# Four edits to the order of work around the second layer of a four-layer graph network

## The chip, the core and the metric

The kernel runs on one core of a Trainium2 chip. The metric is the device time of one execution in microseconds (us); the kernel before takes 2077.56 us (median of three runs, 2076.71 to 2078.34). A core has five engines, each with its own queue of instructions: TensorE (PE, matrix products; its weight loads are listed as PEld), VectorE (DVE), ScalarE (ACT), GpSimd (POOL) and SyncE (SP), which issues most of the transfers (DMAs). [...]

## The reference

Four layers on x of 128 graphs x 64 nodes x 256 features, each followed by a residual sum and a layer normalisation over the features:

```python
x = _layernorm(x + _L0_gnn_ref(x, adj, W, a))             # attention over the adjacency
x = _layernorm(x + _L1_gnn_ref(x, ..., adj, src, dst))    # attention over 512 edges
x = _layernorm(x + _L2_gnn_ref(x, adj, W1, b1, ...))      # the layer of this change
x = _layernorm(x + _L3_gnn_ref(x, adj, Wg0, ..., Wih, Whh, bih, bhh))  # two graph products, then LSTMs
```

Layer 2 (counted from 0) is two dense layers, each with a normalisation over all 8192 rows:

```python
agg = jnp.einsum('nm,bmd->bnd', A_hat, features)
h = jax.nn.relu(_batchnorm(agg.reshape(-1, d) @ W1.T + b1, g1, be1))   # 256 -> 512
out = _batchnorm(h @ W2.T + b2, g2, be2)                               # 512 -> 256
```

## The kernel before, in words

The 8192 rows lie in 16 blocks of 512 (q = 0 to 15), features on the 128 partitions. `Aq(q)` holds a block's input to layer 2 and later half of its hidden values and its result; `Z[q]` holds the other half (`hidden(q, m)`, m = 0 to 3).

*The end of layer 1.* Edge scores of two blocks are gathered in one PSUM bank. `l1_softmax` (line 362) adds a bias, runs two scans for the segment maximum, subtracts and exponentiates (line 375); `l1_sums` (378) runs two more scans; `l1_weights` (383) transposes both results on TensorE (389), takes a reciprocal (395), multiplies (397) and scatters by indirect DMA from GpSimd (401). For the last two blocks these are called one after another after the main loop. `v_a`, `v_b` and `v_c` (410 to 463) then finish layer 1 block by block (line 422 products, 436 output projection, 100 normalisation on GpSimd, 456 neighbour product) while layer 2's first product already fills TensorE (`up`, 737, and `up_job`, 909).

*Jobs of seven products.* Both products of layer 2 are partly done by a scheme of seven products in place of eight (`Seven`, 789). A job covers two blocks and two output parts. It needs sums of its inputs: `tile_sums` (885) and, in a given order, `sums_in_order` (895): t3 on GpSimd, t1 on VectorE in place, t2 and t4 on GpSimd. `factor` (778) says which product uses which. A job's products go in the order 1, 6, 5, 2, 3, 7; the fourth (`tail`, 847) is issued within the next job. `use` (820) takes the products out of PSUM on three engines: lines 823, 827, 829 and 832 ScalarE, 825, 835, 838 and 841 VectorE, 833 and 839 GpSimd. Some products go on in a bank that has just been read (`at`, 803): product 7 waits for line 825, product 4 for line 838, product 2 for line 823, product 3 for line 827. In the second product a job has two terms and so 14 matrix products, each of which is two passes in the profile: 28 passes.

*Statistics and normalisation.* `bn_stats` runs over each finished part; `normalisation` (719) aggregates, takes a reciprocal root by a power on GpSimd (86) and forms scale and shift. `relu` (977) applies them to a block's part in place, on ScalarE.

*The second product.* `first` (1004) does blocks 0 to 3 plainly, k after k, with `beside` (1060) putting rectifications and the sums of blocks 4 and 5 between. Jobs 4, 6, 8, 10 and 12 follow (1090). `prepare(q + 2)` (1021) is stepped through during job q: it rectifies blocks q+2 and q+3 and makes their sums. Blocks 14 and 15 are done plainly at the end (1092 to 1110), and line 1111 adds two bias vectors for the last layer, which come by the transfers of lines 951 and 952.

*The last layer's start.* `gcn` (1216) is a generator for half a group: scale the block (1226), twice transpose, add the residual and normalise (1244, 1250, 100), a neighbour product (1212), two products with the first weights (1282), two with the second (1294) and a last neighbour product whose rectified result goes to `H` (1305 VectorE, 1306 ScalarE). Parts 0 and 1 make the group that the first LSTM step (1331) reads; parts 2 and 3 come after. A list of part numbers (1638) says whose step is issued next.

*What sets the order.* `given` (110) issues what it is handed after the last instruction of each of the four compute engines that was issued through `given` before: it fixes the order of each engine's queue. What isn't issued through it is placed by the scheduler of the framework, by priority and readiness, so that an edit can also move instructions that it does not name.

Of the kernel before, what the change touches and what calls it, by code (L numbers as in the profile page):

```python
# [12 lines left out]
OP = mybir.AluOpType  # L13
# [13 lines left out]
NQ = 16  # L27
# [14 lines left out]
def kernel(ctx: ExitStack, tc: tile.TileContext, i, out):  # L42
    nc = tc.nc
# [66 lines left out]
    def given(do, *args, **more):  # L110
        traced = nc.cur_bb.bb.instructions
        first = len(traced)
        with ExitStack() as order:
            for e in latest.values():
                order.enter_context(tc.issue_after(e))
            r = do(*args, **more)
# [13 lines left out]
    with ExitStack() as two:  # L130
# [355 lines left out]
        ends = su.tile([P, 2, E], F32, name="ends")  # L486
# [195 lines left out]
        for q in range(NQ):  # L682
            S = q // BPS - 1 if q % BPS == 0 else -1
# [15 lines left out]
                    setup.pop(0)()  # L699
        sums(q)  # L700
        S = NQ // BPS - 1
        for do in (l1_softmax, l1_sums, l1_weights):
            do(S)
        ph.close()


# [12 lines left out]
        def normalisation(scale, shift, st, gamma, beta, m):  # L719

            mv = wb.tile([P, 2], F32, name="bn_mv", bufs=4)
            c = slice(m, m + 1)
            nc.vector.bn_aggr(mv, st[:, m, :, :].rearrange("p q s -> p (q s)"))
            rsqrt(scale[:, c], mv[:, 1:2], 1)
            nc.vector.tensor_mul(scale[:, c], scale[:, c], gamma[:, c])
            nc.vector.tensor_mul(shift[:, c], mv[:, 0:1], scale[:, c])
            nc.vector.tensor_sub(shift[:, c], beta[:, c], shift[:, c])
# [123 lines left out]
                if self.done:  # L851
                    self.order(self.done)

        late = []

        def seven(job, feed=iter(())):
            rest = late.pop(0).tail() if late else iter(())
            job.product(1)
            next(feed, None)
            job.product(6)  # L860
            if len(job.terms) > 1:
                next(rest, None)
            next(feed, None)
            job.product(5)
            next(rest, None)
            next(feed, None)
            job.product(2)
            for _ in rest:
                pass
            next(feed, None)  # L870
            job.product(3)
            job.counted(0, 0)
            next(feed, None)
            job.product(7)
            job.counted(0, 1)
            next(feed, None)
            late.append(job)

# [6 lines left out]
        def tile_sums(b):  # L885

            t2, t3, t4 = rooms[next(rooms_at) % len(rooms)]
            t1 = b(0, 1)
            nc.gpsimd.tensor_tensor(t3, b(1, 1), t1, OP.subtract)
            nc.vector.tensor_sub(t1, t1, b(0, 0))  # L890
            nc.gpsimd.tensor_tensor(t2, b(1, 1), t1, OP.subtract)
            nc.gpsimd.tensor_tensor(t4, b(1, 0), t2, OP.subtract)
            return [t1, t2, t3, t4]

        def sums_in_order(b):
# [10 lines left out]
        def inputs(q):  # L906
            return lambda k, n: Aq(q + n)[:, k * QT:(k + 1) * QT]

        def up_job(q, g, T, done=None, **more):
# [3 lines left out]
            seven(Seven([(a, [SW[0][:, n, g] for n in range(4)], inputs(q), T)],  # L913
                        lambda m: b1[:, 2 * g + m:2 * g + m + 1], dst, stats, done, **more))

        T = {}

        def one(q):
            return lambda: up_block(q)
# [12 lines left out]
        q = NQ - LAST - 1  # L932
# [32 lines left out]
        ends = range(NQ - LAST, NQ, 2)  # L965
        T = {ends[0]: tile_sums(inputs(ends[0]))}
# [1 line left out]
        T[ends[1]] = tile_sums(inputs(ends[1]))  # L968

        def finish(g):  # L970
            return lambda: [normalisation(sc1, sh1, st1, g1, be1, 2 * g + m) for m in range(2)]

        for g in range(2):
            for q in ends:
                up_job(q, g, T[q], finish(g) if q == ends[-1] else None, order=given)

        def relu(q, m):
            h = hidden(q, m)
            nc.scalar.activation(h, h, AF.Relu, bias=sh1[:, m:m + 1], scale=sc1[:, m:m + 1])  # L979

        def down(q, m, p_, ks):
            for k in ks:
# [21 lines left out]
        def first(k, feed):  # L1004
            for q in range(LAST):
                for m in range(M2):
                    if k == 0:
                        pz[q, m] = pbank()
                    given(down, q, m, pz[q, m], [k])
                    if k == M1 - 1:  # L1010
                        given(nc.vector.bn_stats, st2[:, m, q, :], pz[q, m])
                        if m:
                            for n in range(M2):
                                given(leave, q, n, pz[q, n])
                    elif k == 0 and m == 0 and q in (0, 1):
                        next(rest, None)
                next(feed, None)

# [18 lines left out]
        def ready(q):  # L1037
            for k in range(M1):
                for n in range(2):
                    given(relu, q + n, k)  # L1040
# [16 lines left out]
        for q in range(LAST):  # L1057
            given(relu, q, 0)

        def beside(k):  # L1060
            q0 = LAST
            early = [(q0 + n, j) for j in (2 * (k // 2), 2 * (k // 2) + 1) for n in range(2)]
            for q in range(LAST):
                if k == 0:
                    given(relu, q, 1)
                if k == 1:
                    given(relu, q, 2)
                    given(relu, q, 3)
                else:
                    if k < 3:  # L1070
# [661 lines left out]
```

## Time and profile before

| what | us |
|---|---|
| time, median of three | 2077.56 |
| the profiled execution: whole | 2077.86 |
| the profiled execution: first to last instruction (span) | 2076.1 |
| end of the last `first` products, start of job 4 (line 813) | 693.77 |
| start of the plain products of blocks 14 and 15 (line 983) | 765.37 |
| the memset of line 1179, the end of layer 2 | 784.17 |
| first LSTM product (line 1331) | 818.61 |

The page of the profile lists busy time per engine; the other views used are busy time in chosen stretches, the waits of one engine in a stretch (engine, tile and line, what it waited for, us in total, times, longest), the chain of waits that ended last (start, us, engine and line), and the timeline (start, us, engine, line, operation, output<-input, count, and in brackets the idle time before with what ended it). A wait is only dear where the waiting engine is the one that the end of the program hangs on.

### The profile page before, as it was taken

The page shows a single profiled execution, that of the slowest core. Times are in us where ns is not written, and L with a number is a line of the kernel's source. Part 1 is how long each engine was busy: PE and PEld are TensorE (multiplying, and loading weights), DVE is VectorE, ACT ScalarE, POOL GpSimd, SP SyncE. Part 2 cuts the span into 40 slices and gives each one's busy share as a digit, 9 for nine tenths or more (in the row PEclk, how much of TensorE's full clock was granted, in tenths as well). Part 3 has the DMA queues.
Part 4 walks back from the last instruction along what each step waited for, and adds up shares of the span by engine and source line. Part 5 has one row for each costly group of instructions (what it writes and reads, how often), then busy time and mean ns, then how long its engine had stood idle before and what let it go on. Part 6 is the DMA issues. An engine that isn't in the chain of part 4 may idle for free.

```text
span 2076.1 us, 31444 instructions
## 1 busy us (share of the span) xinstructions
PE 1964.1 (95%) x11583; PEld 1374.2 (66%) x11583; DVE 1193.1 (57%) x2683; ACT 968.7 (47%) x1852; POOL 809.6 (39%) x961
## 2 busy tenths in 40 slices
PE   5999999998899998999999999999999999999997
PEld 4666667675454335587687587677587677586675
DVE  7455665554556445574456674456674456543556
ACT  2766666665245433443343543343543343543333
POOL 1123343343525434273545243345343345224254
PEclk8999999999999998999999999999999999999998
DMA  5444343332202015451142532032522032301012
GB/s 133 80 66 64 77 77 54 55 54 44 34 21 59 31 71 209 148 192 62 60 153 69 172 121 97 11 126 73 170 95 81 1 113 75 128 1 76 1 60 73
DMA packets 235961, 170.68 MB, mean 82 GB/s; under 512 B 150561, under 2 KB 213537, under 8 KB 232481
## 3 DMA queue, kind: packets, MB, share of 16 engines
q1 hardware_dynamic: 233952, 166.72, 28.6%
q8 instruction: 91, 1.49, 0.3%
q0 software_dynamic: 1024, 1.05, 0.2%
q10 hardware_dynamic: 832, 0.92, 0.1%
q14 instruction: 62, 0.50, 0.1%
HBM read 107.82 MB, written 60.82 MB: 81 GB/s over the span
## 4 chain that ended last, share of the span: by engine, by line
PE 58%; DVE 9%; POOL 4%; issue 2%; ACT 1%; DMA 1%; SPq 0%; POOLq 0%; DVEq 0%; ACTq 0%
PE l L1474 27%; PE l L1439 9%; PE l L1331 8%; PE pz L813 4%; PE pz L742 2%; PE g L1294 2%; PE pz L983 2%; PE g L1212 1%; PE g L1282 1%; DVE cell L1418 1%; DVE gate L1417 1%; DVE ln_st L95 1%; DVE kept L1495 1%; ACT A L979 1%; POOL gate L1497 0%
## 5 line engine op out<-in xcount | busy, mean ns | idle before, releaser
L1474 PE MATMUL l<-xs,wx 128*128 128x256 f32 (+1 forms) x896 | 276.8, 399 | 4.9 <-DVE gate L1493 3.9
L1474 PE MATMUL l<-hs,wh 128*128 128x256 f32 (+1 forms) x896 | 275.0, 399 | 3.1 <-DVE hs L1368 3.1
L86 POOL TENSOR_TENSOR ln_rs<-ln_rs,mhalf 128x2 f32<-128x2 f32 (+2 forms) x98 | 84.0, 858 | 437.2 <-DVE ln_rs L98 425.9
L1489 ACT ACTIVATE kept<-l 128x256 f32<-128x256 f32 (+1 forms) x224 | 88.6, 403 | 339.7 <-PE l L1474 338.5
L1474 PE MATMUL l<-H,wx 128*128 128x256 f32 (+1 forms) x672 | 210.2, 401 | 3.7 <-DVE gate L1502 3.7
L1474 PE MATMUL l<-hid,wh 128*128 128x256 f32 (+1 forms) x672 | 208.7, 399 | 0.0
L1474 PEld LDWEIGHTS l<-xs,wx 128*128 128x128 f32 x896 | 168.8, 190 | 49.3 <-POOL st L100 4.1
L1474 PEld LDWEIGHTS l<-hs,wh 128*128 128x128 f32 x896 | 169.4, 190 | 45.3 <-DVE hs L1368 5.3
L1439 PE MATMUL l<-H,wx 128*128 128x256 f32 (+1 forms) x768 | 187.9, 403 | 6.2 <-DVE H L1404 6.2
L1507 ACT ACTIVATE gate<-gate,bias 128x512 f32<-128x512 f32 (+1 forms) x280 | 170.7, 657 | 37.1 <-DVE gate L1498 31.1
L1439 PEld LDWEIGHTS l<-H,wx 128*128 128x128 f32 x768 | 146.8, 193 | 46.4 <-DVE H L1404 10.4
L1331 PE MATMUL l<-H,wih 128*128 128x512 f32 x384 | 167.9, 598 | 2.6 <-issue 2.6
L357 ACT ACTIVATE u<-z 128x1024 f32<-128x1024 f32 x128 | 130.4, 1025 | 63.3 <-PE z L355 62.3
L1474 PEld LDWEIGHTS l<-H,wx 128*128 128x128 f32 x672 | 126.0, 190 | 38.6 <-DVE gate L1502 7.6
L1474 PEld LDWEIGHTS l<-hid,wh 128*128 128x128 f32 x672 | 127.2, 190 | 32.0 <-issue 2.6
L1331 PEld LDWEIGHTS l<-H,wih 128*128 128x128 f32 x384 | 73.3, 192 | 93.2 <-issue 86.2
L1497 POOL TENSOR_TENSOR gate<-gate,kept 128x256 f32<-128x256 f32 (+1 forms) x84 | 65.1, 775 | 159.1 <-DVE kept L1495 159.1
L329 DVE TENSOR_TENSOR qs<-m,qs 64x256 fp32r<-64x256 f32 x128 | 54.0, 422 | 109.7 <-ACT qs L328 107.6
L1372 POOL TENSOR_TENSOR hs<-hid 128x256 f32<-128x256 f32 (+1 forms) x28 | 26.0, 930 | 200.2 <-DVE hid L1401 116.3
L355 PE MATMUL z<-gath_r,qs 128*128 128x512 f32 x256 | 99.9, 478 | 0.1
L1426 ACT ACTIVATE gate<-cell 128x512 f32<-128x512 f32 (+1 forms) x88 | 58.6, 666 | 81.0 <-DVE cell L1418 57.5
L1491 DVE TENSOR_TENSOR gate<-l,kept 128x256 f32<-128x256 f32 (+1 forms) x112 | 49.1, 438 | 71.4 <-ACT gate L1507 43.7
(340 smaller groups left out, 3831.4 us busy)
## 6 DMA issues: line engine op xcount, KB each, us to landing
wx<-sums SPq DMA_DIRECT2D x9, 2048.0 KB
wh<-sums SPq DMA_DIRECT2D x9, 1792.0 KB
way<-st SPq DMA_DIRECT2D x54, 256.0 KB
st<-way SPq DMA_DIRECT2D x216, 64.0 KB
xin<-in_x SPq DMA_DIRECT2D x16, 512.0 KB
ld<-table SPq DMA_DIRECT2D x16, 512.0 KB
x_dram<-y SPq DMA_DIRECT2D x16, 512.0 KB
x2r<-x_dram SPq DMA_DIRECT2D x32, 256.0 KB
```

What stands on the lines that cost most here:

```text
L86: nc.gpsimd.tensor_tensor(dst, dst, mhalf[:, :n], OP.pow)
L329: nc.vector.tensor_sub(qs[ro, s, :], pq[r, :D], qs[r, s, :].bitcast(F32))
L355: nc.tensor.matmul(z[:, k, :], L1[q]["qs"][c][:, s, k * P:(k + 1) * P], gath_r, start=True, stop=True)
L357: nc.scalar.activation(u, z, AF.Relu)
L813: nc.tensor.matmul(self.bank[at], lhs, rhs, start=first and n == 0, stop=n == len(self.terms) - 1, skip_group_check=True)
L1331: nc.tensor.matmul(b, wih1[:, k, mw * P:(mw + 1) * P], Hw[:, k], start=k == 0, stop=k == KD - 1)
L1426: nc.scalar.activation(tiles["g"][m], cell[:, m], AF.Tanh)
L1439: nc.tensor.matmul(one, w.raw[0][:, k, at, m, :], inp(r, 0, k)[:, g], start=k == 0, stop=k == KD - 1)
L1474: nc.tensor.matmul(self.banks[j], lhs, rhs, start=src == 0, stop=src == 1)
L1489: nc.scalar.activation(self.keep(j), b, AF.Copy)
L1497: e.tensor_tensor(t[0][:, 1], t[0][:, 1], k[5], OP.add)
L1507: given(lambda: nc.scalar.activation(dst, dst, f, bias=b))
```

## The change

1. The last `l1_softmax` and `l1_sums` are issued through `given`, and so are the four instructions of `tile_sums`; so the softmax stands ahead of the input sums.
2. `normalisation` is made of two parts, `variance` (aggregate, root) and `affine` (scale and shift). For the first product's statistics, `finish` no longer runs them at once but puts the parts of two columns into a list, `aside`, from which `two_aside` issues two at a time at later points.
3. Rectifications: those of blocks 0 to 3, part 0, move into the last `up_job`; `prepare(q)` now makes the sums of blocks q and q+1 and rectifies blocks q+2 and q+3, so rectifications are two jobs ahead; those of blocks 6 and 7 move into `beside`. `ready` is gone.
4. The list that orders the steps of parts 0 to 3 in the last layer changes.

```diff
-        for do in (l1_softmax, l1_sums, l1_weights):
-            do(S)
+        given(l1_softmax, S)
+        given(l1_sums, S)
+        l1_weights(S)
...
+        def halves(scale, shift, st, gamma, beta, m):
             mv = wb.tile([P, 2], F32, name="bn_mv", bufs=4)
             c = slice(m, m + 1)
+            return [lambda: variance(mv, scale[:, c], st, m), lambda: affine(mv, scale, shift, gamma, beta, c)]
+
+        def variance(mv, dst, st, m):
             nc.vector.bn_aggr(mv, st[:, m, :, :].rearrange("p q s -> p (q s)"))
-            rsqrt(scale[:, c], mv[:, 1:2], 1)
+            rsqrt(dst, mv[:, 1:2], 1)
+
+        def affine(mv, scale, shift, gamma, beta, c):
             nc.vector.tensor_mul(scale[:, c], scale[:, c], gamma[:, c])
...
+        def two_aside():
+            for part in aside[:2]:
+                given(part)
+            del aside[:2]
...
             job.counted(0, 0)
+            two_aside()
             next(feed, None)
             job.product(7)
             job.counted(0, 1)
+            two_aside()
...
-            nc.gpsimd.tensor_tensor(t3, b(1, 1), t1, OP.subtract)
-            nc.vector.tensor_sub(t1, t1, b(0, 0))
-            nc.gpsimd.tensor_tensor(t2, b(1, 1), t1, OP.subtract)
-            nc.gpsimd.tensor_tensor(t4, b(1, 0), t2, OP.subtract)
+            given(nc.gpsimd.tensor_tensor, t3, b(1, 1), t1, OP.subtract)
+            given(nc.vector.tensor_sub, t1, t1, b(0, 0))
+            given(nc.gpsimd.tensor_tensor, t2, b(1, 1), t1, OP.subtract)
+            given(nc.gpsimd.tensor_tensor, t4, b(1, 0), t2, OP.subtract)
...
         def finish(g):
-            return lambda: [normalisation(sc1, sh1, st1, g1, be1, 2 * g + m) for m in range(2)]
+            def done():
+                both = [halves(sc1, sh1, st1, g1, be1, 2 * g + m) for m in range(2)]
+                aside.extend(h[n] for n in range(2) for h in both)
+            return done
...
+        def early_relus():
+            yield
+            for q in range(LAST):
+                yield
+                given(relu, q, 0)
...
-                    elif k == 0 and m == 0 and q in (0, 1):
+                    elif k == 0 and m == 0 and q < 3:
                         next(rest, None)
...
+            later = [(k, n) for k in range(M1) for n in range(2)]
+
+            def one():
+                k, n = later.pop(0)
+                given(relu, q + 2 + n, k)
             for g in range(2):
-                for k in range(2):
-                    for n in range(2):
-                        given(relu, q + n, 2 * g + k)
-                    if k == 0:
-                        yield
...
                 T = sums_in_order(b)
-                yield next(T)
+                next(T)
+                one()
+                yield
                 terms[q].append((a, [SW[1][:, n, g] for n in range(4)], b, next(T)))
+                one()
                 if g == 0:
-                    yield
+                    one()
                 yield
+            one()
+            yield
+            one()
+            one()
...
+                if k >= 2:
+                    given(relu, q0 + 2 + q % 2, 2 * (k - 2) + q // 2)
+                two_aside()
...
-            down_job(q, prepare(q + 2) if q + 2 < NQ - 2 else ready(q + 2))
+            down_job(q, prepare(q + 2) if q + 2 < NQ - 2 else iter(()))
...
-    for n in [0, 0, 0, 1, 0, 1, 0, 1, 0, 1, 0, 1, 2, 0, 1, 0, 1, 3, 1, 2, 2, 1, 3, 3]:
+    for n in [0, 0, 0, 1, 1, 0, 1, 0, 0, 1, 0, 0, 1, 1, 0, 2, 1, 3, 1, 1, 2, 2, 3, 3]:
```

More of the change, by code (lines that the diff above doesn't have):

```diff
@@ L717, with normalisation @@
         sc2, sh2 = (const.tile([P, M2], F32, name=n) for n in ("sc2", "sh2"))
-        def normalisation(scale, shift, st, gamma, beta, m):
+        def normalisation(*args):
+            for part in halves(*args):
+                part()
+        def halves(scale, shift, st, gamma, beta, m):
             mv = wb.tile([P, 2], F32, name="bn_mv", bufs=4)
             c = slice(m, m + 1)
+            return [lambda: variance(mv, scale[:, c], st, m), lambda: affine(mv, scale, shift, gamma, beta, c)]
+        def variance(mv, dst, st, m):
             nc.vector.bn_aggr(mv, st[:, m, :, :].rearrange("p q s -> p (q s)"))
-            rsqrt(scale[:, c], mv[:, 1:2], 1)
+            rsqrt(dst, mv[:, 1:2], 1)
+        def affine(mv, scale, shift, gamma, beta, c):
             nc.vector.tensor_mul(scale[:, c], scale[:, c], gamma[:, c])
@@ L852, in tail @@
                     self.order(self.done)
-        late = []
+        late, aside = [], []
+        def two_aside():
+            for part in aside[:2]:
+                given(part)
+            del aside[:2]
         def seven(job, feed=iter(())):
@@ L907, in inputs, with up_job @@
             return lambda k, n: Aq(q + n)[:, k * QT:(k + 1) * QT]
-        def up_job(q, g, T, done=None, **more):
+        def up_job(q, g, T, done=None, feed=iter(()), **more):
             a = lambda m, k: w1[:, k, (2 * g + m) * P:(2 * g + m + 1) * P]
@@ L913, in up_job @@
             seven(Seven([(a, [SW[0][:, n, g] for n in range(4)], inputs(q), T)],
-                        lambda m: b1[:, 2 * g + m:2 * g + m + 1], dst, stats, done, **more))
+                        lambda m: b1[:, 2 * g + m:2 * g + m + 1], dst, stats, done, **more), feed)
         T = {}
@@ L970, in finish @@
         def finish(g):
-            return lambda: [normalisation(sc1, sh1, st1, g1, be1, 2 * g + m) for m in range(2)]
-        for g in range(2):
-            for q in ends:
-                up_job(q, g, T[q], finish(g) if q == ends[-1] else None, order=given)
+            def done():
+                both = [halves(sc1, sh1, st1, g1, be1, 2 * g + m) for m in range(2)]
+                aside.extend(h[n] for n in range(2) for h in both)
+            return done
         def relu(q, m):
@@ L979, in relu @@
             nc.scalar.activation(h, h, AF.Relu, bias=sh1[:, m:m + 1], scale=sc1[:, m:m + 1])
+        def early_relus():
[3 more added lines that the diff above has]
+                given(relu, q, 0)
+        for g in range(2):
+            for q in ends:
+                last = q == ends[-1]
+                up_job(q, g, T[q], finish(g) if last else None, feed=early_relus() if last and g else iter(()),
+                       order=given)
         def down(q, m, p_, ks):
@@ L1031, in prepare @@
                 T = sums_in_order(b)
-                yield next(T)
+                next(T)
+                one()
+                yield
                 terms[q].append((a, [SW[1][:, n, g] for n in range(4)], b, next(T)))
+                one()
                 if g == 0:
-                    yield
[L1037 to L1040, printed above, removed]
+                    one()
                 yield
+            one()
+            yield
+            one()
+            one()
         def down_job(q, feed):
@@ L1056 @@
         rest = late.pop(0).tail()
-        for q in range(LAST):
-            given(relu, q, 0)
         def beside(k):
```

## The prediction, made before the changed kernel ran

> **What bounds the kernel now.** I read the page first, then the busy times by stretch, then what TensorE waited for in each stretch of layer 2, then the chain of waits through one job, and last the timelines around single places.
>
> ```profile
> PE 1964.1 (95%) x11583; PEld 1374.2 (66%) x11583; DVE 1193.1 (57%) x2683; ACT 968.7 (47%) x1852; POOL 809.6 (39%) x961
> ```
>
> TensorE is the bound, and the change removes no product: the order of the built programs shows the same matrix products, a few of them in another place. So it can only win or lose idle TensorE time, and the slow matmuls that follow idle time. Busy time by stretch (us, each engine, then the granted clock) says where that lies:
>
> ```profile
> 520.00:560.00 40.00, 31.76 (x215) 16.05 (x216) 21.10 (x35) 10.18 (x16) 20.93 (x20) 0.96 0.25 39
> ...
> 695.00:725.00 30.00, 25.79 (x56) 10.77 (x54) 17.52 (x26) 18.04 (x27) 17.84 (x15) 0.94 0.12 48
> 725.00:755.00 30.00, 26.26 (x56) 11.06 (x56) 15.22 (x20) 14.56 (x22) 16.94 (x15) 0.94 0.15 62
> ...
> 785.00:820.00 35.00, 28.24 (x338) 19.52 (x337) 22.09 (x61) 13.07 (x22) 10.77 (x18) 0.84 0.66 232
> ```
>
> 8.2 us idle around the last softmax, some 4 us in each 30 us of the second product's jobs, 6.8 us in the first blocks of the last layer, all with the clock below 1. The waits of TensorE (us in total, times, longest) in the stretches 518 to 665, 665 to 784 and 784 to 880 name the causes:
>
> ```profile
> PE m L389 <- ACT e L375: 4.9, 1, 4.9
> PE m L456 <- POOL y L100: 2.2, 2, 1.5
> PE pz L813 <- DVE wq L838: 1.9, 1, 1.9
> ...
> PE pz L813 <- POOL wv L116: 4.4, 2, 2.2
> PE pz L813 <- POOL Z L116: 4.4, 2, 2.2
> PE pz L983 <- ACT Z L979: 0.6, 1, 0.6
> ...
> PE l L1331 <- issue: 2.6, 1, 2.6
> ```
>
> The four waits of 2.2 us are one per job. The chain of waits through one of them (start, us):
>
> ```profile
> 717.15 0.44 ACT A L829
> 717.59 0.15 issue
> 717.74 2.93 ACT A L979 x4
> 720.66 0.07 issue
> 720.73 1.28 POOL seg L116
> 722.01 0.02 issue
> 722.04 1.75 DVE A L116
> 723.79 0.07 issue
> 723.86 1.28 POOL wv L116
> ```
>
> Four rectifications, then GpSimd, VectorE and GpSimd by turns, and only then TensorE: the next job's sums start when this job is nearly over.
>
> [...] after two of the four 2.2 us waits the next 14 matmul passes take 7.99 us, after the other two 6.29 us, where the undisturbed pace is 0.429 us each (6.0 us). [...] the in-place subtraction takes 0.69 us alone and 1.74 us beside the GpSimd sum of line 839.
>
> **The change part by part.** Times are on the clock of the profiled run (span 2076.1, whole run 2077.86 us).
>
> *Last softmax.* Before, VectorE runs the first scan to 526.09, then sits 1.77 us behind a subtraction of the input sums (527.86, waiting for GpSimd's lb), then the second scan (1.22), then a subtraction of 1.57 us beside GpSimd; the exponential ends at 531.95. In the changed order that subtraction stands behind both softmax scans and their sums. Second scan 526.1 to 527.4, subtraction 0.69 to 1.1, exponential 0.63: about 529.0, so the first transposes come 3.0 us earlier. The further scans (1.23, 1.22) put the next transposes at about 531.4 against 534.52, and the reciprocal, which stood behind the second input subtraction, at 532.7 against 537.40. Against it: two of the GpSimd sums (1.27 each) and two scatters (about 1.07 each) now stand before or between the normalisation of block 12, so TensorE, which also gets 4 more passes before it, waits longer there: 2 us at about 542 instead of 1.5. The normalised block ends near 545.7 instead of 547.7, and of the later passes 4 fewer remain (1.7 us). At the products of line 422 (553.5 before) that makes 3.6 us earlier; bounds 2.0 (GpSimd sums at the 2.04 to 2.18 us they took beside VectorE) and 4.4. TensorE is busy without a break from there to 615, and the scores that it needs next land at 562.6 for use at 580, so the gain is kept.
>
> *Normalisation in two parts.* Before, ten small VectorE instructions (655.57 to 659.4), two of them waiting for GpSimd, stand before line 838, and TensorE waits 1.85 us for it. Now only the aggregates and additions, 1.3 us, stand ahead, and the product it guards is 0.9 us further on. Gain 1.85 plus 0.2 of slow matmuls: 2.1.
>
> *The bias sum moves too.* The order of VectorE shows a side effect: line 1111 stood after line 841 and idled there; now eight others stand behind it, the last input subtraction among them. It waits for a transfer:
>
> ```profile
> L952 SPq DMA_DIRECT2D bias<-in_L_gnn_bhh x1: 3998/3998/3998, 630.6 to 630.6; - x1
> L1111 DVE TENSOR_TENSOR bias<-bias,bias x1: 192/192/192, 638.5 to 638.5; 128x32 f32<-128x32 f32 x1
> ```
>
> VectorE reaches it at 633.0 and is held to 638.5. Then come the sum itself (0.2), six statistics (0.63 each), line 841 (0.75), the subtraction (0.69) and line 825 (0.66), which so ends at 644.6 against 641.7. The seventh product, at 643.21 before, waits for it: 1.4 us lost. Bounds: 0 (if the transfer gains on TensorE) and 3.0 (the subtraction at 1.74 us and a slow clock). The DMA queue order ahead of it is unchanged, so it moves with the rest.
>
> *Early rectifications.* The first four leave the start of the second product: its 0.6 us wait and 0.1 of slow matmul go. ScalarE has room: 16.5 us busy of 30, and eight more at 0.71 make 22. Gain 0.7 (0 to 0.8).
>
> *Jobs.* From 693.77 to 765.37 five jobs of 28 passes took 71.6 us; at 0.429 us they need 60.1. The new order has the sums of job q+2 wait for nothing of ScalarE's in job q. I walked it: GpSimd does 7 x 1.27 = 8.9 us per job, ScalarE 11 x 0.71 = 7.8, VectorE about 7 to 8, all below 12.0. The last sum that TensorE needs in the following job's second product ends at 706.6 where it is wanted at 706.7 after the first job (VectorE is late there with lines 993), and some 1.2 us ahead in later ones. The subtraction and the sums before and after it depend on each other, so they do not overlap and keep 0.69 and 1.27. The subtraction now stands before lines 835 and 838, which delays 838 by about 2 us; its reader, the fourth product, comes 1.2 us after that. Gain 11.5; bounds 8 and 11.9.
>
> *First blocks of the last layer.* The critical end is this pair in the timeline:
>
> ```profile
> 817.51 1.00 DVE L1305 TENSOR_SCALAR H<-l 128x512 f32<-128x512 f32 x1
> ...
> 818.61 7.08 PE L1331 MATMUL l<-H,wih 128*128 128x512 f32 x12 [2.63 <-issue]
> ```
>
> Line 1305 stood behind two normalisations of part 2; now it stands ahead of them. Walking the new order from 784.2 with the rows' durations: part 1's first transposes fill the wait at 787; its products of line 1212 end at 797.5 instead of 801.1; line 1294 starts at 798.5, the last products of line 1212 at 811.4, line 1305 ends at 813.7, and line 1331 starts at 814.3, 4.3 us earlier. What is late next: part 3's normalisation, whose chain on VectorE begins at 813.7 as before, ending at 823.1 on GpSimd; its products follow at once, ending 4.2 us before the old 827.65. Bounds 2.5 (an extra stall of each of two new ones, 0.95 and 0.45 us found on the walk, and a cold clock) and 5.5. The loads of the second residual blocks now come after six stores but before both weights, so they arrive in time.
>
> Sum: -3.6 - 2.1 + 1.4 - 0.7 - 11.5 - 4.3 = -20.8. The profiled run took 2077.86, 0.3 above the median of the three: 2057.1 for it, 2056.8 for the median. The LSTM's order after 830 is the same, and its TensorE full there, so I expect the gain to stay.
>
> **Rivals.** A, the jobs keep a wait: VectorE's subtraction before line 835 leaves a stall of about 1 us in each of four jobs and the clock drops after half of them, 4 + 2.5: 2063. For it: no margin at the first handover. Against: 1.2 us later. B, the last layer returns 1 us rather than 4.3, since parts 2 and 3 normalise no earlier: 2060. C, VectorE's hold for the bias costs its full 5.4 us instead of 1.4: 2061. D, the slower one: the pulled-forward sums run beside VectorE work[...], so that the job's chain of seven GpSimd sums at 2.04 and two subtractions at 1.74 becomes the bound: 17.8 us per job, 89 against 71.6, +17.4 - 9.3 = 8 us slower, 2086. It decides from 16.2 us per job on. Against it: in the jobs before, the sums took 1.27. E, a part doesn't do what it says: the orders show all of them moved, so this only has a share in "no change".
>
> **How the numbers follow.** Forecast 0.55, A 0.20, B 0.13, C 0.07, D 0.03, no change 0.02. The forecast's own bounds give about 2053 to 2061; reaching to A and B makes 2053 to 2063.5. About 0.2% (4 us) is what can be told from no change: faster 0.95, within 0.02, slower 0.03.
>
> **What would show it.** Right: line 813 waiting for no line 116; jobs 12.0 us apart at clock 1; line 375 near 529; line 838's wait gone; VectorE idle some 5 us before the bias sum and a TensorE wait of about 1.4 us on line 825; line 1331 starting some 30 us after line 1179. Wrong: sums of line 116 at 2 us, TensorE waiting for line 838 or 835 in the jobs, or the gain lost to new waits after line 1331.

## The result, and the profile after

The changed kernel takes 2061.01 us (median of four runs, 2059.52 to 2064.21), the kernel before in the same set 2077.25: ratio 0.9923, 95% interval 0.9906 to 0.9940, so 16 us less. The profiled execution of the changed kernel is the longest of its four, 2064.21 us with a span of 2062.3; against the profiled execution before the span falls by 13.8 us.

In the code after the change lines have moved: 813 is now 822, 825 is 834, 838 is 847, 983 is 1010, 1179 is 1209, 1212 is 1242, 1282 is 1312, 1305 and 1306 are 1335 and 1336, and 1331 is 1361. The sums of `tile_sums` now go through `given` and are listed under its line 116. The first line of the page, and then four stretches that answer to those of before (busy us of TensorE, its weight loads, VectorE, ScalarE, GpSimd, then the granted clock; the last stretch starts 0.5 us after the end of layer 2, the one shown of before 0.8):

```profile
PE 1962.4 (95%) x11583; PEld 1374.8 (67%) x11583; DVE 1187.8 (58%) x2683; ACT 968.4 (47%) x1852; POOL 810.8 (39%) x961
```

```profile
520.00:560.00 40.00, 32.52 (x215) 16.70 (x216) 21.10 (x35) 9.77 (x16) 20.17 (x20) 0.91 0.34 43
695.00:725.00 30.00, 30.00 (x71) 13.22 (x70) 17.78 (x30) 19.82 (x29) 21.89 (x18) 1.00 0.17 70
725.00:755.00 30.00, 30.00 (x71) 13.09 (x70) 15.10 (x24) 12.55 (x19) 15.75 (x13) 1.00 0.18 72
771.00:806.00 35.00, 32.30 (x348) 21.65 (x349) 21.80 (x58) 14.43 (x25) 9.72 (x17) 0.86 0.62 225
```

The number of products is the same. In the jobs (second and third line) TensorE has no idle time left and a clock of 1.00. Around the last softmax (first line) it is busy 32.5 of 40 us where it was 31.8, but at a clock of 0.91 in place of 0.96: more busy time that is not more work. What TensorE waited for in the changed kernel (us in total, times, longest), in 518 to 660, 660 to 762 and 762 to 830:

```profile
PE m L456 <- POOL y L100: 4.1, 2, 3.3
PE m L389 <- ACT e L375: 2.9, 1, 2.9
...
PE pz L822 <- DVE kept L834: 1.0, 1, 1.0
...
PE pz L822 <- DVE wq L847: 0.9, 1, 0.9
...
PE g L1211 <- DVE st L1209: 3.3, 1, 3.3
PE g L1242 <- POOL A L100: 2.5, 2, 1.7
PE l L1242 <- POOL A L100: 1.7, 2, 1.4
```

All four waits on line 116 are gone. The wait for the exponential is 2 us shorter, but the one for block 12's normalisation (`y`) has grown from 1.5 to 3.3 us. The wait on line 834 is new. In the last layer the 2.6 us before the first LSTM product are gone, while those of line 1242 add up to 4.4 us (0.2 of it, for VectorE, is not in the lines above) where they were 4.1. The chain of waits through the jobs shows how complete that part is, 136 passes in a row at 0.429 us each:

```profile
693.53 58.37 PE pz L822 x136
751.90 0.86 PE pz L1010 x2
752.76 1.91 PE pz L822 x4
```

And among VectorE's own waits (625 to 650 us) stands the transfer of the bias vector:

```profile
DVE bias L1141 <- DMA bias<-in_L_gnn_bhh: 5.5, 1, 5.5
```

**How to compare runs of this kernel.** The executions of one kernel differ by several us, in places that no edit touches. So each profile was cut, by starts in TensorE's timeline, into stretches: up to the first 16 matmuls of line 346 after 498 us ("lead"); from there to the last group of line 422, near 552 ("softmax"); to the 30 plain matmuls of line 1010 near 666 ("first product"); 12.87 us, the same in all; from the next 32 plain matmuls to the memset of line 1209 ("jobs"); from there to the last eight matmuls g<-hT,wg of line 1312, near 818 ("last layer"); and the rest. In us, with the median of the runs and the interval of its ratio to the kernel before in the same set (the kernels are described below):

| kernel | lead | softmax | first product | jobs | last layer | rest | median (lowest to highest, runs) | ratio, 95% |
|---|---|---|---|---|---|---|---|---|
| before | 503.4 | 50.1 | 113.7 | 104.1 | 48.7 | 1243.2 | 2077.25 to 2078.96, medians of four sets | 1 |
| changed | 503.0 | 50.6 | 113.2 | 90.9 | 48.3 | 1243.5 | 2061.01 (2059.52 to 2064.21, 4) | 0.9906 to 0.9940 |
| again | 503.2 | 49.0 | 113.1 | 90.9 | 46.9 | 1242.3 | 2061.14 (2060.09 to 2063.27, 5) | 0.9912 to 0.9938 |
| again_b | 503.1 | 49.0 | 113.2 | 90.9 | 46.8 | 1242.8 | 2061.55 (2060.64 to 2062.81, 5) | 0.9906 to 0.9932 |
| old_softmax | 499.1 | 52.3 | 111.8 | 90.9 | 47.6 | 1242.2 | 2059.44 (2058.89 to 2062.14, 5) | 0.9907 to 0.9932 |
| old_halves | 501.8 | 51.5 | 114.2 | 90.9 | 45.1 | 1239.9 | 2061.23 (2058.34 to 2067.87, 6) | 0.9910 to 0.9937 |
| old_relus | 501.5 | 51.5 | 113.0 | 102.4 | 45.0 | 1244.1 | 2069.82 (2065.56 to 2076.68, 12) | 0.9956 to 0.9978 |
| old_list | 503.2 | 50.9 | 113.0 | 90.9 | 49.9 | 1240.3 | 2060.89 (2060.60 to 2063.21, 5) | 0.9911 to 0.9937 |
| norm_first | 500.7 | 47.7 | 112.4 | 90.9 | 47.9 | 1242.1 | 2058.43 (2056.71 to 2058.66, 4) | 0.9886 to 0.9917 |
| bias_last | 501.3 | 50.8 | 111.8 | 91.1 | 45.0 | 1239.4 | 2058.21 (2054.26 to 2063.22, 5) | 0.9893 to 0.9920 |
| parts_between | 502.7 | 50.7 | 113.3 | 90.9 | 46.0 | 1240.7 | 2058.37 (2057.65 to 2060.43, 4) | 0.9887 to 0.9917 |
| two_edits | 499.2 | 47.8 | 111.8 | 91.1 | 48.3 | 1242.9 | 2055.90 (2052.45 to 2057.00, 4) | 0.9872 to 0.9901 |
| two_old_list | 499.2 | 47.8 | 111.8 | 91.1 | 48.5 | 1243.2 | 2059.48 (2056.25 to 2060.72, 5) | 0.9893 to 0.9918 |
| all_three | 501.3 | 48.4 | 111.8 | 91.1 | 46.5 | 1241.1 | 2055.01 (2053.15 to 2055.38, 4) | 0.9867 to 0.9897 |

The reader is to see three kinds of column. "First product" and "jobs" repeat to 0.35 us wherever the same order runs, so an edit of 0.5 us shows there. "Softmax" and "last layer" scatter by 2.6 and 3.3 us with one and the same order. Lead and rest scatter by 4.3 and 4.7 us although no edit lies in them. Part of the scatter of "softmax" lies ahead of what the edits move: its first 20.3 to 22.6 us, up to the first softmax instruction on VectorE (line 367). From there to the last group of line 422 the kernel before and old_softmax, which share the order, take 29.8 and 29.7 us, and the eight profiles with the order of the change 28.2 to 30.3, mean 28.9. This "way from line 367" is given below beside the stretch.

### The profile page after: what moved, and what is told of

It reads as the page before. It is cut to its first block, busy times and chain, and to the rows that moved or that the text cites. A ratio compares the mean times of both kernels' runs of the same rounds, so it can differ in the third digit from the quotient of the medians.

```text
span 2062.3 us, 31449 instructions
## 1 busy us (share of the span) xinstructions
PE 1962.4 (95%) x11583; PEld 1374.8 (67%) x11583; DVE 1187.8 (58%) x2683; ACT 968.4 (47%) x1852; POOL 810.8 (39%) x961
## 4 chain that ended last, share of the span: by engine, by line
PE 59%; DVE 9%; POOL 3%; issue 1%; DMA 1%; ACT 1%; SPq 0%; POOLq 0%; DVEq 0%
PE l L1504 27%; PE l L1469 9%; PE l L1361 8%; PE pz L822 4%; PE g L1324 2%; PE pz L751 2%; PE pz L1010 2%; PE g L1312 1%; PE g L1242 1%; DVE cell L1448 1%; DVE gate L1447 1%; DVE ln_st L95 1%; DVE kept L1525 1%; POOL gate L1527 0%; DVE gate L1523 0%
```

## The experiments

**again** is the changed kernel unedited.

> The changed kernel once more, for its spread: four runs lay from 2059.5 to 2064.2 us, the profiled one at 2064.2. Theory P[...]: the waits of TensorE come out within 0.3 us of the first profile, and what differs is the pace of the products after the long waits: the 8 passes of line 751 after the normalised block (5.87 us in the first profile, 3.44 at full clock), the 8 of line 1312 (5.6 against 3.44) and the 12 of line 1361 (6.74 against 5.15). Together up to 6 us, so runs from about 2058.5 to 2064.5. Rival: the waits themselves differ (the transfer of the bias lands elsewhere, the block normalises earlier), by 2 us or more.

2061.14 us. The timeline of TensorE behind the same wait, first in the changed kernel's profile, then in that of again:

```profile
545.53 2.33 PE L456 MATMUL m<-aht,y 64*64 64x64 f32 x64 [3.33 <-POOL y L100]
547.78 5.87 PE L751 MATMUL pz<-A,w 128*128 128x512 f32 x8
```

```profile
545.70 2.32 PE L456 MATMUL m<-aht,y 64*64 64x64 f32 x64 [3.34 <-POOL y L100]
547.95 4.28 PE L751 MATMUL pz<-A,w 128*128 128x512 f32 x8
```

The waits agree to 0.01 us, and the eight matmuls behind them take 5.87 or 4.28 us (3.60 for the eight from 523.07 in the changed kernel, where nothing disturbed them). The granted clock goes with it: over 520 to 560 us it is 0.91 in the first profile, with 0.62 over these eight matmuls, and 0.96 in the second. So a wait has a price of its own and a second that differs from run to run, here 0.7 to 2.3 us. What sets the second was not shown.

**old_relus** (part 3 undone: rectifications one job ahead, those of blocks 0 to 3 at the start of the second product, those of blocks 6 and 7 out of `beside`):

```diff
+                for k in range(2):
+                    for n in range(2):
+                        given(relu, q + n, 2 * g + k)
+                    if k == 0:
+                        yield
...
-            down_job(q, prepare(q + 2) if q + 2 < NQ - 2 else iter(()))
+            down_job(q, prepare(q + 2) if q + 2 < NQ - 2 else ready(q + 2))
```

> The changed kernel with the rectifications as before, one job ahead and with the sums behind them. Theory 1: the jobs' stretch is the whole gain, 13.2 us by the traces (136 passes at 0.429 us instead of 71.6 us), and the early rectifications another 0.7: about 2061 + 14 = 2075, with the four waits of 2.2 us on line 116 back. Rival: the prediction's 11.5 + 0.7 = 12.2, 2073; or, if the other parts carry half of the gain, 2069.

2069.82 us, 8.7 above again. That is well below what the expectation's theory (2075) and its rival (2073) said, and close to its last case (2069), in which other parts carry half of the gain. TensorE's timeline of old_relus has the four waits back:

```profile
707.90 1.12 PE L822 MATMUL pz<-Z,SW 128*128 128x512 f32 x2 [2.19 <-POOL Z L116]
...
753.02 1.12 PE L822 MATMUL pz<-wv,SW 128*128 128x512 f32 x2 [2.21 <-POOL wv L116]
```

and its chain of waits the pace behind them:

```profile
722.37 6.29 PE pz L822 x14
...
736.84 7.99 PE pz L822 x14
```

Four waits are 8.8 us; the slow matmuls behind them add 2.7 here (102.4 against 90.9 in the jobs), 4.4 in the profile before. So part 3 is worth 8.8 us in waits and a few more, not the same in every run, in slow matmuls; the median difference of the runs, 8.7, would leave almost nothing for the slow matmuls, although the profiled run (2072.32) has them. Why the median lies so low is open. Its twelve runs spread over 11 us, those of the changed kernel over 5 at most, but this cannot be put down to the four waits: two kernels below without them, old_halves and bias_last, spread over 9.5 us in six runs and 9.0 in five. In the first product, however, undoing the early rectifications changes nothing (113.0 against 113.2): the 0.6 us wait for line 994 is back, and the 0.9 us wait for line 847 that stands there in the changed kernel is gone. One takes the place of the other.

**old_softmax** (part 1 undone):

```diff
-        given(l1_softmax, S)
-        given(l1_sums, S)
-        l1_weights(S)
+        for do in (l1_softmax, l1_sums, l1_weights):
+            do(S)
```

with the four sums of `tile_sums` out of `given` too.

> The changed kernel with the softmax and the input sums as before (not through the ordered issue). My prediction gave this part 3.6 us. Theory 1, from the two traces: the 3 us won at the exponential are lost again where the normalised block 12 waits behind two sums and three scatters on GpSimd, so undoing it costs nothing: within 1.5 us of the changed kernel, 2059.5 to 2062.5, and it may gain up to 2.4 when the clock stays up; and the bias sum goes back behind line 841, which gives about 1.4 to 2.2 us back: 2058.5 to 2060. Rival (the prediction): 3.6 slower less 1.4, about 2063.

2059.44 us, 1.7 below again, with intervals that overlap. Two effects stand against each other. Its softmax stretch is 52.3 us, longer than any of the eight with the changed order there (49.0 to 51.5, mean 50.5), but 2.3 us of this lie ahead of line 367. The way from line 367 is 29.7 us against a mean of 28.9, so that part 1 wins 0.8 us there. The first product is 1.4 us shorter, since without this part the sum of the bias vectors keeps its place behind line 850 and holds nothing. Part 1 as a whole brought this kernel nothing that can be seen in its time.

**norm_first** tests why the earlier exponential won so little. GpSimd's timeline of the changed kernel, up to block 12's normalisation (line 100):

```profile
533.33 1.27 POOL L116 TENSOR_TENSOR gath<-A 128x512 f32<-128x512 f32 x1 [5.04 <-DVE A L116]
534.68 1.27 POOL L116 TENSOR_TENSOR keep<-A,gath 128x512 f32<-128x512 f32 x1
535.91 1.27 POOL L116 TENSOR_TENSOR seg<-A 128x512 f32<-128x512 f32 x1
537.35 1.51 POOL L401 DMA_INDIRECT table<-at,place  x1 [0.17 <-issue]
538.89 1.28 POOL L116 TENSOR_TENSOR wv<-A 128x512 f32<-128x512 f32 x1
540.34 0.99 POOL L401 DMA_INDIRECT table<-at,place  x1 [0.16 <-issue]
541.35 1.28 POOL L116 TENSOR_TENSOR w<-A,wv 128x512 f32<-128x512 f32 x1
542.58 1.06 POOL L86 TENSOR_TENSOR ln_rs<-ln_rs,mhalf 128x4 f32<-128x4 f32 x1
543.82 1.04 POOL L401 DMA_INDIRECT table<-at,place  x1 [0.19 <-issue]
544.92 2.18 POOL L100 TENSOR_SCALAR y<-y,ln_rs 128x256 f32<-128x256 f32 x4
```

The same places in the kernel before, and after them the instruction of VectorE that hands over the normalisation's input (line 98) in the changed kernel:

```profile
538.91 1.27 POOL L892 TENSOR_TENSOR w<-A,wv 128x512 f32<-128x512 f32 x1
...
543.71 0.16 DVE L98 TENSOR_SCALAR ln_rs<-ln_mv 128x4 f32<-128x4 f32 x1
...
545.53 2.17 POOL L100 TENSOR_SCALAR y<-y,ln_rs 128x256 f32<-128x256 f32 x4
```

```profile
540.58 0.16 DVE L98 TENSOR_SCALAR ln_rs<-ln_mv 128x4 f32<-128x4 f32 x1
```

Before, the same five sums ended at 540.18, well ahead of the input at 543.71. In the changed kernel they waited until 533.3 for VectorE, which now does the softmax first, and then ran in a bunch with three scatters: the input is there at 540.58, but the last sum runs until 542.63, and the third scatter comes between the reciprocal root (line 86) and `y`. Measured from the first softmax instruction on VectorE (line 367, at 523.73 before and 523.27 changed), the input comes 2.7 us earlier and `y` 0.15. The edit issues the first step of the normalisation in the fixed order, so that the sums stand behind it:

```diff
-            do(q, *[False] * (do == v_c))
+            (given if n == 0 else lambda do, *args: do(*args))(do, q, *[False] * (do == v_c))
```

> Theory Q (a queue on GpSimd took the softmax gain): with the changed kernel the first transposes of the last softmax come 2.5 us earlier, but block 12's normalisation now stands behind two input sums and three scatters on GpSimd, so the neighbour product of line 456 waits 3.3 us and the matmuls behind it lose pace. Here the first input sum is held behind that normalisation. Expected: the wait of line 456 on y under 1 us, the products of line 422 starting at 549.5 to 551 instead of 552.2 to 553.6, run 2057 to 2059.5. Rival (the gain is bounded by the scatters and the transposes, not by the queue): line 422 unmoved within 0.5 us, another wait in its place, run 2060 to 2062. Third possibility: the held input sums come late for the third part's first job, so that what is won at 550 is given back by 640: line 422 earlier, run 2060 to 2062.

2058.43 us, in the expected range. GpSimd's timeline of norm_first, and after it TensorE's:

```profile
539.37 1.04 POOL L86 TENSOR_TENSOR ln_rs<-ln_rs,mhalf 128x4 f32<-128x4 f32 x1
540.52 2.16 POOL L100 TENSOR_SCALAR y<-y,ln_rs 128x256 f32<-128x256 f32 x4
...
543.97 1.28 POOL L116 TENSOR_TENSOR lb<-A 128x512 f32<-128x512 f32 x1
```

```profile
541.13 2.07 PE L456 MATMUL m<-aht,y 64*64 64x64 f32 x64 [1.02 <-POOL y L100]
543.13 5.42 PE L751 MATMUL pz<-A,w 128*128 128x512 f32 x12
548.48 1.16 PE L422 MATMUL m<-am,v 64*64 64x64 f32 x64
```

The wait is 1.0 us in place of 3.3, and the twelve matmuls of line 751 behind it take 5.42 us, where twelve before the wait take 5.31 in the changed kernel (from 536.88). Line 422 starts at 548.48, before the expected range, but 2.2 us of that are a shorter lead. The edit also does a second thing: with no sum on GpSimd beside the subtraction before the exponential (line 374; GpSimd is idle from 526.2 to 535.4), TensorE waits 2.0 us for the exponential in place of 2.9, and the input subtractions no longer stand ahead in VectorE's queue. The normalisation's input is ready by 539.37, where line 86 starts, in place of 540.74, so of the 4.4 us by which `y` starts earlier 1.4 or a little more come from VectorE and some 3 from GpSimd's queue. In four kernels with this edit the softmax stretch is 47.7 to 48.4 us, mean 47.9, against 50.5: 2.6 us shorter. The way from line 367 is 25.1 to 25.2 us in three of them and 27.1 in all_three, against 28.9: 3.3 us shorter on average, and in the three 4.6 shorter than in the kernel before. The sums came in time for the jobs that read them: the first product does not grow. Theory Q holds, with this help from VectorE.

**bias_last** puts the bias sum behind layer 2's last instructions:

```diff
-        nc.vector.tensor_add(bias, bias, bias2)
+        given(nc.vector.tensor_add, bias, bias, bias2)
```

> The sum of the two last-layer bias vectors is held behind layer 2's last instructions on VectorE. Theory (it stands in VectorE's queue, waits there for its transfer and holds line 834, which costs TensorE 1.0 us of waiting and some pace): the wait on kept of line 834 and the 0.9 us on wq of line 847 go or shrink, the plain products of line 928 start 1 to 2.2 us earlier against line 422, run 2058.8 to 2060. Rival (the product behind it waits for another engine at the same time): wait replaced by another, distance from line 422 to line 928's first product within 0.4 us of the changed kernel's, run 2060.5 to 2062.

2058.21 us, 3 below the changed kernel in the other sets, with intervals that overlap; of that the place explains 1.4: the first product takes 111.8 us in each of the four kernels with this edit, 113.0 to 113.3 with the sum in front (112.4 in norm_first, where the wait for line 834 was only 0.3 us). Among its waits of TensorE in 600 to 680 there is none for line 834, and this one for line 847:

```profile
PE pz L822 <- DVE wq L847: 1.0, 1, 1.0
```

That wait stays, so it was not the bias sum's. VectorE's timeline of bias_last shows what stands before it:

```profile
657.35 1.04 DVE L734 TENSOR_TENSOR sc<-sc,g 128x1 f32<-128x1 f32 x1
...
659.08 0.16 DVE L736 TENSOR_TENSOR sh<-be,sh 128x1 f32<-128x1 f32 x1
659.16 0.69 DVE L834 TENSOR_TENSOR kept<-pz,kept 128x512 f32<-128x512 f32 x1
...
660.42 1.87 DVE L928 BATCH_NORM_STATS2 st<-A 128x6 f32<-128x512 f32 x3
662.21 0.68 DVE L847 TENSOR_TENSOR wq<-pz,kept 128x512 f32<-128x512 f32 x1
```

The second half of the normalisation, 1.8 us from 657.35, no longer stands before the first line 847 but in the queue before the next one. That it makes that one late is read from this order; no run moved it again.

**old_halves** (part 2 undone):

```diff
-                both = [halves(sc1, sh1, st1, g1, be1, 2 * g + m) for m in range(2)]
-                aside.extend(h[n] for n in range(2) for h in both)
-            return done
+            return lambda: [normalisation(sc1, sh1, st1, g1, be1, 2 * g + m) for m in range(2)]
```

> Change part 2 undone: the first product's normalisation runs at once again, ten small instructions in a row. Theory (the halves took away the 1.85 us wait that stood at line 838 of the kernel before, and about 1.9 us in all together with the early rectifications): that wait is back at line 847, and the distance from line 422's last group to the 30 plain matmuls of blocks 0 to 3, 113.2 us in the changed kernel, becomes 114.4 to 115.2; run 1 to 2 us slower than the changed kernel. Rival (the bias sum's stall in the same queue covers it): the distance within 0.4 us of 113.2, run unchanged.

The wait for line 847 is 1.8 us again, and the first product 114.2 us, 1.0 longer: more than the rival's 0.4, a little less than the theory's 114.4. The time (2061.23 against 2061.55 for again_b in the same set) shows no loss; 1 us drowns in its scatter.

**old_list** (part 4 undone: the list of part numbers of before) and **two_old_list** (the same on top of the two edits that helped):

```diff
-    for n in [0, 0, 0, 1, 1, 0, 1, 0, 0, 1, 0, 0, 1, 1, 0, 2, 1, 3, 1, 1, 2, 2, 3, 3]:
+    for n in [0, 0, 0, 1, 0, 1, 0, 1, 0, 1, 0, 1, 2, 0, 1, 0, 1, 3, 1, 2, 2, 1, 3, 3]:
```

> The changed kernel with the old order of the steps in the last layer. My prediction gave this part 4.3 us. Theory 1, from the traces: the first LSTM product starts 2.9 us earlier but the products of part 3 then wait 1.4 us for its normalisation and the clock is half for one stretch more, so the part is worth 0.5 us: 2060 to 2062.5. Rival (the prediction): 4.3 slower, about 2065.

> As two_edits, but with the list of parts of the kernel before (change part 4 undone). Theory (the change's list takes 2.5 us of idle TensorE time out of the stage[...]): idle time in the stage from line 1209 to the last eight matmuls of line 1312 back from 7.1-7.7 to about 10 us, run 1 to 3 us slower than two_edits. Rival (the list is worth nothing, since its wait is only replaced by a slower pace): run within 0.7 us of two_edits.

The two answers differ: 0.25 us below again for the first, 3.6 above two_edits (2055.90) for the second. Nor do the profiles of that second pair hold the 3.6: their last-layer stretches differ by 0.2 us. The profiles agree on the idle time. TensorE's waits of two_old_list in 762 to 815:

```profile
PE g L1211 <- DVE st L1209: 3.4, 1, 3.4
PE g L1242 <- POOL A L100: 2.8, 2, 2.5
PE l L1361 <- issue: 2.3, 1, 2.3
PE l L1242 <- POOL A L100: 1.1, 1, 1.1
```

That is 9.6 us, where the changed kernel has 7.7 and two_edits 7.8. In the whole stretch it is 9.6 to 10.0 us in the three profiles with the old list and 6.9 to 7.8 in the nine with the new one: the list takes out 2 to 3 us of idle time. The stretch itself takes 48.5 to 49.9 us in three profiles with the old list (mean 49.0) and 45.0 to 48.3 in nine with the new one (mean 46.8): 2.3 us on average, with a scatter that is larger. The size of this part is known only to some 2 us.

**parts_between** puts the normalisations of parts 2 and 3 between part 1's steps:

```diff
-    for n in [0, 0, 0, 1, 1, 0, 1, 0, 0, 1, 0, 0, 1, 1, 0, 2, 1, 3, 1, 1, 2, 2, 3, 3]:
+    for n in [0, 0, 0, 1, 1, 0, 1, 0, 0, 1, 2, 0, 2, 0, 2, 1, 3, 1, 0, 1, 3, 1, 1, 3]:
```

> Only the list of part numbers is different: the normalisations of parts 2 and 3 are issued between part 1's steps, the result of part 1 stays ahead of part 3's last normalisation. Theory (rival B of the prediction: the last layer's stage is bounded by the chain of VectorE and GpSimd normalisations of parts 2 and 3, which the change leaves as late as before): the 1.4 us wait of line 1242 and the slow matmuls of line 1312 behind it go, the stage from line 1209 to the eight matmuls of line 1312 of part 3 shrinks from 48.4 to 45.5 to 47 us, run 2058 to 2060. Other side (the list only says who waits: total idle is set by work on VectorE and GpSimd together): line 1361 starts later by what the other wait saves, stage 48 to 49 us, run 2060.5 to 2062.5.

The 1.4 us wait is gone, and these of its waits in 762 to 815 have grown or are new:

```profile
PE g L1242 <- POOL A L100: 2.8, 2, 2.1
PE l L1324 <- ACT xs L1316: 0.8, 1, 0.8
PE l L1361 <- ACT H L1336: 0.6, 1, 0.6
PE l L1242 <- DVE st L1327: 0.5, 1, 0.5
```

Idle time is 8.6 us, more than 7.7, and the stretch takes 46.0 us (46.5 in all_three), as the nine others do. Its run was 2058.37 all the same, but no stretch that the list touches holds those 3 us; together with the other two edits it adds 0.9 us, less than the runs scatter. That it helps was not shown.

**two_edits** (norm_first and bias_last together) and **all_three** (with parts_between as well):

> The first input sum behind block 12's normalisation and the bias sum behind layer 2, with the change's own list of parts. Theory (each acts at its own place): line 422 at 548 to 550, distance to the 30 plain matmuls 111.7 to 112, run 2055.5 to 2057.5. If the new list of the set before (parts 2 and 3 between) has no effect of its own, it equals all_three's 2055.0 within 1 us; if that list has the 2.5 us it seemed to have alone, this is 2 us slower than all_three.

> The three edits together (first input sum behind block 12's normalisation, bias sum behind layer 2, parts 2 and 3 between). If each acts where it was aimed and nothing later takes it back, they add up: 2053 to 2056. If only one of them acts: 2058 to 2060. If they meet in one queue, above all GpSimd's at 545 to 600, the sum is smaller than the parts.

2055.90 us (0.9886, 0.9872 to 0.9901) and 2055.01 us (0.9882, 0.9867 to 0.9897) are below both kernels, with intervals that do not reach the changed kernel's. In two_edits softmax is 47.8 and the first product 111.8 us, the values of its two parts: they add. That is 5 to 6 us below the changed kernel, of which the way from line 367 holds 3.8 and the first product 1.4. **again_b**, the baseline of the third set:

> The changed kernel unedited, as the baseline beside the next three on the same chip. Expected: ratio to the kernel before as in the first two sets, 0.992 to 0.993, run 2059.5 to 2062.5. If it comes out at 0.990 instead, the gains of the single edits of the second set were those of the chip or the hour and not of the edits.

0.9919 (0.9906 to 0.9932), as in the first two sets, and two_edits stands 5.7 us below it on the same chip: the gain of the pair is not the chip's. The second set itself had no run of the changed kernel beside its single edits, so these rest on their own stretches.

## Why the prediction was right, and where its sum was off

The forecast of 2056.8 us had the direction and the main mechanism; the time came out 4.2 us higher, at the upper edge of the forecast's own bounds (about 2053 to 2061). The miss would have been 1.7 us larger if the largest term had not been too small by that much. The time is also the 2061 of rival C, but by coincidence: the bias sum cost 1.4 us, not the 5.4 of that rival. By the steps of the sum:

| step | predicted | measured | from |
|---|---|---|---|
| last softmax | -3.6 | -0.8 (from +0.6 to -1.5) | way from line 367: 29.8 and 29.7 with the old order, mean of eight 28.9 |
| normalisation in halves | -2.1 | -1.0 beside the bias sum, up to -1.9 without | first product of old_halves; of before and bias_last |
| bias sum | +1.4 | +1.4 | bias_last |
| early rectifications | -0.7 | 0 (0.1 the other way) | first product of old_relus |
| jobs | -11.5 | -13.2 (-11.5 by the profile, -8.7 by the runs of old_relus) | jobs, before and changed |
| last layer | -4.3 | -2.3 (-0.5 by the first pair) | means of three and nine |

Right: the jobs, with their cause. TensorE waits for no sum, VectorE's subtraction ahead of line 844 leaves no stall, and the sums keep their 1.27 to 1.28 us, so rival A and the slower rival D fell. The term was 1.7 us too small for a slip in counting: the stretch held 136 passes, not 140 (58.4 us, not 60.1); the other four are issued among the plain products. The bias sum's side effect was read from VectorE's order and cost what it was said to, as a wait on line 834 of 1.0 us and what follows.

Failed: the step of the last softmax. Its 3.6 us were 2.0 for an earlier `y`, behind "two of the GpSimd sums" and two scatters, and 1.7 for four passes fewer after it. The 2.0 did not come at all: `y` starts 21.6 to 22.0 us after line 367 in the eight profiles with the changed order, and 21.8 before. Five sums stood ahead of it in both kernels. What changed is when they run: VectorE held them until 533.3, and then they came all at once, just when the earlier softmax needed GpSimd. The transposes after the exponential came 2 us earlier rather than 3, since the scan of line 373 and the subtraction of line 374 took 1.57 us each where 1.3 and 0.69 to 1.1 were put down (line 374 took 1.57 in the kernel before too, both times beside a GpSimd sum, of 2.04 and 2.17 us; an input subtraction of the same size with GpSimd idle, at 532.52 in the changed kernel, took 0.67), and these 2 us were won and lost again at line 456. The 1.7 came whole only in old_list and bias_last, where `y` to line 422 took 6.2 us against 8.0 before; in the others slow matmuls behind the wait took some or all of it back (7.0 to 8.7 us). norm_first, which moves `y` forward by 4.5 us, shows that the queue on GpSimd was the larger reason.

Mis-sized: the halves took away the wait that was named, but the next line 847 was then late by 0.9 us, by the order of the queue because of the moved half, and this also took the place of the rectification's 0.6 us; that is why the two terms together gave 1.9 at most (113.7 before, 111.8 in bias_last) in place of 2.8, and with the bias sum's 1.4 a net of 0.5 in place of 1.4. In the last layer the 2.6 us before the LSTM went, as walked: its first product starts 29.8 to 31.4 us after the end of layer 2 in the nine profiles with the new list, where the walk had 30.1 and the kernel before has 34.4. But parts 2 and 3 normalise no earlier, and part 3's products then waited 1.4 us: rival B had the mechanism, on average not its full size.

Open: by the stretches (-0.8, -0.5, -13.2, -2.3) the change is worth 16.8 us, by the runs of the three sets 16.2 to 17.4. They agree, but two of the four terms carry a scatter of 2 to 3 us. The parts do not add up in the time when each is undone alone in the changed kernel: part 3 is worth 8.7 us, while old_softmax, old_halves and old_list are 0.2 to 1.7 us faster than their baselines. That makes 6.4 of 16.3 us, and the times do not say where the other 10 are; the interval of each ratio is nearly 3 us to either side. The exact worth of the list was not settled.

## What to carry to other kernels

When a step is moved ahead in one queue, list what it was moved past and find when that work now runs: held-back work arrives in a bunch, on another engine, just when something that is waited for needs that engine, even if the order of its queue hardly changes. Judge an edit of 1 or 2 us by the length of its own stretch between two fixed points, over all profiles that share the order there, and not by the time of the whole. A wait that ends often lets the next one show at the same place, so price a removed wait by the distance to the next engine that is late.

## What the runs showed that was not expected

Waits of 2.2 us brought slow matmuls, but not each time and not at the same places. Behind the first three of the four waits 14 passes took 7.99, 6.29 and 7.99 us in the kernel before and 6.29, 6.29 and 7.99 in old_relus; the 22 passes behind the last took 9.71 in both, where 0.429 us a pass make 6.0 and 9.4. In the kernel before the granted clock is 0.79 over each of the two stretches of 7.99 us, and 1.00 over those of 6.29 and 9.71. So a wait of 2.2 us can cost more than itself in this kernel; from which length on a wait does so was not shown.

The runs of one kernel also scatter without such waits: bias_last lay between 2054.26 and 2063.22 us, old_halves between 2058.34 and 2067.87.
